# Masked attention with residual norms on one core: the softmax denominators' sums issued in each block's own step, y in two buffers, the norm's small product on GpSimd

## The chip, the core and the metric

The kernel runs on one core of a Trainium2 chip. A core has five engines that run side by side: TensorE (PE in the profile, its weight loads PEld), VectorE (DVE), ScalarE (ACT), GpSimd (POOL) and SyncE (SP, which only issues DMAs here). Each takes its instructions in the order of its queue, and an instruction that waits holds all behind it. DMA transfers are issued by SP or by GpSimd and run on 16 DMA engines. The metric is device time in microseconds, the median of three runs.

## The reference

For each of 8 frames of 2048 nodes with 256 channels the kernel computes eight-head attention (heads of 32) under an adjacency mask that all frames share, and then three layer norms with residuals and a two-layer network between them:

```python
qkv = jnp.einsum('fnc,ck->fnk', x, w_qkv)
scores = jnp.einsum('fnhd,fmhd->fhnm', q, k) / jnp.sqrt(D)
scores = jnp.where(adj > 0, scores, -1e9)
attn = jax.nn.softmax(scores, axis=-1)
t = jnp.einsum('fhnm,fmhd->fnhd', attn, v).reshape(F, N, C)
x1 = layernorm(x + t) * ln1_g + ln1_b
h = jax.nn.relu(x1 @ w1 + b1)
x2 = layernorm(x1 + h @ w2 + b2) * ln2_g + ln2_b
out = layernorm(x + x2)
```

All of it is float32.

## The kernel before

**Tiling.** A frame's queries are cut into four chunks `qc` of 512, the eight heads into two groups `g` of four, and the keys into 16 blocks `mb` of 128. One item `(f, qc, g, mb)` is one *block step*: there are 8 x 4 x 2 x 16 = 1024, unrolled in that order (L362). A *group* is the 16 steps of one `(f, qc, g)`. `tc.manual_schedule()` keeps every engine's instructions in the order in which the Python code makes them.

**A block step** `t` does four things, in this order. `advance(t)` puts one piece of waiting fill work in front (two where `mb` is odd, none where `mb` is 0). `scores(items[t + 2])` (L169) works two steps ahead: matmuls into PSUM, transposed, keys on the partitions; DVE adds the mask and writes the block's tile `p` (128 x 4 heads x 512 queries, 1 MB) to SBUF (L180); ACT takes exp in place (L182). `values(items[t])` (L186) adds this block's part of attention times V to a PSUM bank. Last, `denominators(t)` (L205) issues what the softmax denominators need. The pool `pp` has nine slots for `p`; a slot comes free when all that reads the tile has ended.

**Denominators before.** The sum over keys goes over partitions and over 16 blocks. Blocks 0 to 13 of a group make seven pairs: two steps after the even block, a DMA issued by GpSimd adds its tile onto the odd one's (L211); five steps after, GpSimd adds the pair to `acc` (the first two pairs make it, L218, the others L220: six additions). Blocks 14 and 15 stay as they are. `denominator` (L243), started five steps after block 15, contracts the three terms with a matrix of ones (L250), copies the result (L252), transposes it (L256), and takes the reciprocal (L260); L265 and L266 keep a running sum and minimum of the reciprocals, which at the end decide whether a slower, general path has to be run.

**The fill.** Work other than attention is written as generators that `yield` the number of steps to wait; `advance` runs the first that is due, and a generator that yields 0 lets the next one go. Denominators and tails are put at the head of the list (`urgent`), projections of the next frame and, in frame 0, the turning of the mask at its end. Where K and V of the next frame are not ready when its scores are due, the loop at L381 drives the fill until they are.

**The tail** of a query chunk (L268) runs from `state["y"]` being clear to its store: attention is transposed and divided into the tile `y` (L279, L280), x is added by a DMA that GpSimd issues (L284), three steps later comes a norm, then transposes (L294), the first layer (L303), the second (L312) with DVE's addition (L314), a norm, GpSimd's scaling (L317, L318), x again (L319), a norm, and the store (L322, on SP's queue). `state["y"]` is cleared once the store has been issued. `y` has one buffer.

**The norm** (L223): DVE takes mean and variance (L227, L228); GpSimd computes `rs`, one over the root of variance plus eps, in two small operations (L231, L232); two steps later DVE computes `nb = -mean * rs` (L235), and ACT normalizes in place with four activations (L237).

Of the kernel before, what the change touches and what calls it, by code (L numbers as in the profile page):

```python
# [10 lines left out]
F32 = mybir.dt.float32  # L11
# [4 lines left out]
ALU = mybir.AluOpType  # L16
AX = mybir.AxisListType

P = 128
H = 8  # L20
D = 32
CH = 512
# [1 line left out]

RS_MIN = 1e-19
RS_MAX = 1e25

MASKED = -57344.0  # L30

# [21 lines left out]
def fast_path(ctx, tc, cst, x, adj, out, RS):  # L53
    nc = tc.nc
    F, N, C = x.shape
    NCK, TPC, MB = N // CH, CH // P, N // P
# [7 lines left out]
    pp = ctx.enter_context(tc.tile_pool(name="pp", bufs=9))  # L64
    ap = ctx.enter_context(tc.tile_pool(name="ap", bufs=1))
    work = ctx.enter_context(tc.tile_pool(name="work", bufs=1))
    op = ctx.enter_context(tc.tile_pool(name="op", bufs=1))
    small = ctx.enter_context(tc.tile_pool(name="small", bufs=4))

# [97 lines left out]
    PT, O, OT, DT, ACC, RC = {}, {}, {}, {}, {}, {}  # L167
# [16 lines left out]
    LAST = MB - 1  # L184
# [14 lines left out]

    NPAIR = MB // 2 - 1
    ISSUE, ADD, SUM = 2, 5, 20

    def denominators(t):  # L205
        def block(back):
            return items[t - back] if 0 <= t - back < len(items) else (0, 0, 0, LAST)
        item = block(ISSUE)
        f, qc, g, mb = item
        if mb % 2 == 0 and mb // 2 < NPAIR:  # L210
            nc.gpsimd.dma_start(PT[f, qc, g, mb + 1], PT.pop(item), accum_op=ALU.add)  # L211
        f, qc, g, mb = block(ADD)
        grp, k = (f, qc, g), mb // 2
        if mb % 2 == 0 and 0 < k < NPAIR:
            pair = PT.pop((f, qc, g, mb + 1))
            if k == 1:
                ACC[grp] = ap.tile([P, 4, CH], F32, name="acc")
                nc.gpsimd.tensor_tensor(ACC[grp], PT.pop((f, qc, g, 1)), pair, ALU.add)  # L218
            else:
                nc.gpsimd.tensor_tensor(ACC[grp], ACC[grp], pair, ALU.add)  # L220


    def norm(t):  # L223
        mv = small.tile([P, TPC, nc.vector.BN_AGGR_DIM], F32, name="mv")
        for j in range(TPC):
            st = small.tile([P, nc.vector.BN_STATS_DIM], F32, name="st")
            nc.vector.bn_stats(st, t[:, j, :])  # L227
            nc.vector.bn_aggr(mv[:, j, :], st)  # L228
        yield 1
        rs = small.tile([P, TPC], F32, name="rs")  # L230
        nc.gpsimd.tensor_scalar(rs, mv[:, :, 1], EPS, 1.0, op0=ALU.add, op1=ALU.mult)  # L231
        nc.gpsimd.tensor_tensor(rs, rs, cst["mhalf"], ALU.pow)  # L232
        yield 2
        nb = small.tile([P, TPC], F32, name="nb")
        nc.vector.scalar_tensor_tensor(nb, mv[:, :, 0], -1.0, rs, op0=ALU.mult, op1=ALU.mult)  # L235
        for j in range(TPC):
            nc.scalar.activation(t[:, j, :], t[:, j, :], AF.Identity, bias=nb[:, j:j + 1], scale=rs[:, j:j + 1])  # L237
        yield 1
# [3 lines left out]

    def denominator(f, qc, g):  # L243
        grp = (f, qc, g)
        terms = [PT.pop((f, qc, g, LAST - 1)), PT.pop((f, qc, g, LAST)), ACC.pop(grp)]
        ps = bank()
        for n, term in enumerate(terms):
            for h in range(4):
                r = D * h
                nc.tensor.matmul(ps[r:r + D, :], cst["ones"], term[:, h, :], start=(n == 0), stop=(n == 2))  # L250
        dT = op.tile([P, CH], F32, name="dT")
        nc.scalar.copy(dT, ps)  # L252
        yield 1
        ps = bank()
        for j in range(TPC):
            nc.tensor.transpose(ps[:, j * P:(j + 1) * P], dT[:, j * P:(j + 1) * P], ident)  # L256
        if g == 0:
            RC[f, qc] = op.tile([P, TPC, H], F32, name="rc")
        rc = RC[f, qc]
        nc.vector.reciprocal(rc[:, :, 4 * g:4 * g + 4], ps.rearrange("p (j c) -> p j c", c=P)[:, :, ::D])  # L260
        if g == 0:
            return
        start(items.index((f, qc, g, LAST)) + SUM - MB + 3, tail(f, qc), urgent=True)
        rcf = rc.rearrange("p j h -> p (j h)")
        nc.vector.tensor_tensor(RS[:, 0, :], RS[:, 0, :], rcf, ALU.add)  # L265
        nc.vector.tensor_tensor(RS[:, 1, :], RS[:, 1, :], rcf, ALU.min)  # L266

    def tail(f, qc):  # L268
        while state["y"]:
            yield 0  # L270
        state["y"] = True
        rc = RC.pop((f, qc))
        xin = x[f, qc * CH:(qc + 1) * CH, :].rearrange("(j p) c -> p j c", p=P)
        y = work.tile([P, TPC, C], F32, name="y")
        for gg in range(2):
            oT = OT.pop((f, qc, gg))
            ps = bank()
            for j in range(TPC):
                nc.tensor.transpose(ps[:, j * P:(j + 1) * P], oT[:, j * P:(j + 1) * P], ident)  # L279
            nc.vector.tensor_tensor(y[:, :, gg * P:(gg + 1) * P].rearrange("p j (h d) -> p j h d", d=D),  # L280
                                    ps.rearrange("p (j h d) -> p j h d", h=4, d=D),
                                    rc[:, :, 4 * gg:4 * gg + 4, None].to_broadcast([P, TPC, 4, D]), ALU.mult)
            yield 1
        nc.gpsimd.dma_start(y, xin, accum_op=ALU.add)  # L284
        yield 3
        yield from norm(y)
        while state["turned"]:
            yield 0
        state["turned"] = True
        yT = work.tile([P, 2, CH], F32, name="turned")  # L290
        for a in range(2):
            ps = bank()
            for j in range(TPC):
                nc.tensor.transpose(ps[:, j * P:(j + 1) * P], y[:, j, a * P:(a + 1) * P], ident)  # L294
            nc.scalar.activation(yT[:, a, :], ps, AF.Identity, bias=cst["be1c"][:, a:a + 1], scale=cst["g1c"][:, a:a + 1])  # L295
            yield 1
        nc.gpsimd.tensor_tensor(y, y, rows(cst["g1r"]), ALU.mult)
        nc.gpsimd.tensor_tensor(y, y, rows(cst["be1b2r"]), ALU.add)
        hT = work.tile([P, 2, CH], F32, name="hT")
        for d in range(2):  # L300
            ps = bank()
            for a in range(2):
                nc.tensor.matmul(ps, w1s[:, a, d * P:(d + 1) * P], yT[:, a, :], start=(a == 0), stop=(a == 1))  # L303
            nc.scalar.activation(hT[:, d, :], ps, AF.Relu, bias=cst["b1s"][:, d:d + 1], scale=1.0)  # L304
            yield 1
        state["turned"] = False
        z = y
        for jj in range(0, TPC, 2):
            ps = bank()
            for j in range(jj, jj + 2):  # L310
                for d in range(2):
                    nc.tensor.matmul(ps[:, (j - jj) * C:(j - jj + 1) * C], hT[:, d, j * P:(j + 1) * P], w2s[:, d, :],  # L312
                                     start=(d == 0), stop=(d == 1))
            nc.vector.tensor_tensor(z[:, jj:jj + 2, :], ps.rearrange("p (b c) -> p b c", c=C), z[:, jj:jj + 2, :], ALU.add)  # L314
            yield 1
        yield from norm(z)
        nc.gpsimd.tensor_tensor(z, z, rows(cst["g2r"]), ALU.mult)  # L317
        nc.gpsimd.tensor_tensor(z, z, rows(cst["be2r"]), ALU.add)  # L318
        nc.gpsimd.dma_start(z, xin, accum_op=ALU.add)  # L319
        yield 5  # L320
        yield from norm(z)
        nc.sync.dma_start(out[f, qc * CH:(qc + 1) * CH, :].rearrange("(j p) c -> p j c", p=P), z)  # L322
        state["y"] = False
# [4 lines left out]
    def start(t, gen, urgent=False):  # L328
        fill.insert(0 if urgent else len(fill), [t, gen])
# [32 lines left out]
    for t, (f, qc, g, mb) in enumerate(items):  # L362
# [20 lines left out]
                t0 += 1  # L383
            scores(items[t + LEAD])
        values(items[t])
        denominators(t)
        if mb == LAST:
            start(t + SUM - MB + 1, denominator(f, qc, g), urgent=True)
    t = len(items)
    for i in range(ADD):  # L390
        denominators(t + i)
    while fill:
        t += 1
        advance(t)
# [125 lines left out]
def kernel(  # L520
# [15 lines left out]
    nc = tc.nc  # L536
    F, N, C = x.shape
    assert C == H * D == 2 * P and N % CH == 0
    NCK, TPC = N // CH, CH // P
# [32 lines left out]
    nc.gpsimd.memset(cst["ones"], 1.0)  # L572
    cst["mhalf"] = const.tile([P, TPC], F32, name="mhalf")
    nc.gpsimd.memset(cst["mhalf"], -0.5)
    RS = const.tile([P, 2, TPC * H], F32, name="RS")
    nc.gpsimd.memset(RS[:, 0, :], 0.0)
    nc.gpsimd.memset(RS[:, 1, :], 1.0)

    fast_path(tc, cst, x, adj, out, RS)

# [1 line left out]
    with tc.tile_pool(name="gd", bufs=1) as gd, \  # L582
            tc.tile_pool(name="gdp", bufs=1, space=bass.MemoryType.PSUM) as gdp:
        ok = gd.tile([P, 2], F32, name="ok")
        nc.vector.tensor_reduce(ok[:, 0:1], RS[:, 0, :], AX.X, ALU.add)
        nc.vector.tensor_reduce(ok[:, 1:2], RS[:, 1, :], AX.X, ALU.min)
        nc.vector.tensor_scalar(ok[:, 0:1], ok[:, 0:1], RS_MAX, None, op0=ALU.is_le)
        nc.vector.tensor_scalar(ok[:, 1:2], ok[:, 1:2], RS_MIN, None, op0=ALU.is_ge)
        ps = gdp.tile([2, 1], F32, name="okp")
        nc.tensor.matmul(ps, ok, cst["ones"][:, 0:1], start=True, stop=True)  # L590
        n_ok = gd.tile([2, 1], F32, name="nok")
# [39 lines left out]
```

## Time and profile before

| | |
|---|---|
| three runs | 4570.1, 4572.4, 4586.9 us; median 4572.44 |
| the profiled execution | 4558.5 us, its span 4556.7 us |
| granted TensorE clock in it, mean | 0.898 |
| first exp starts | 73.8 us |
| last exp starts | 4464.8 us |
| DMA queue that GpSimd issues to | 503.35 MB, 56.0% of 16 engines' span |

In the page's busy rows an engine's time is given as a share of the span. Rows of slices cut the span into 40 equal parts, a digit for each, in tenths; PEclk is the granted TensorE clock. In the answers on waits a row reads: engine, tile and line that waited, what ended the wait, total us, times, longest. In the groups of instructions: line, engine, operation, tiles, shapes, count, then busy us and mean ns, then the idle time before them and what ended most of it. A timeline row has the start in us, the duration, engine, line, tiles, count of merged instructions, and in brackets the idle time of the engine just before and what ended it. The answer on a single line has min/median/max of its durations in ns.

### The profile page before, as it was taken

Reading aid. Unit: us, or ns where it says so; the run is one execution under the profiler, and the core shown is the slowest. Engines: PE = TensorE matmul, PEld = TensorE weight load, DVE = VectorE, ACT = ScalarE, POOL = GpSimd, SP = SyncE. Lnnn points to the kernel's source line nnn. Section 1 sums busy time; section 2 is a strip of 40 time slices with the busy share of each in tenths; the row PEclk is TensorE's granted clock in tenths of the full one; section 3 lists DMA queues with packets and bytes.
Section 4 is the critical chain, followed back from the end, with each engine's and each line's share of the span. In section 5 each row is a group of like instructions: output and inputs, shape, how many; then the busy total and the mean of one; then the engine's idle time right before and its main releaser. Section 6 shows DMA issues by size and latency. Waiting matters only on the chain. (4 is left out here: it accounts for less than half of the span.)

```text
span 4556.7 us, 51690 instructions
## 1 busy us (share of the span) xinstructions
PE 3456.5 (76%) x20996; PEld 1038.2 (23%) x20996; DVE 2881.5 (63%) x3207; ACT 2458.0 (54%) x1953; POOL 2640.3 (58%) x1227
## 2 busy tenths in 40 slices
PE   7777778777777777777877777877778777787773
PEld 3122222212222222222221122221222222222221
DVE  3867547776476764766647765477655776567672
ACT  4665546555465554555545555455554555455552
POOL 1565546665466664765646755466645666456664
PEclk9998999889998899888998889898898988998886
DMA  5875756666476664776646765467754676556663
GB/s 145 177 156 131 155 105 123 135 140 143 101 144 140 123 139 99 145 149 135 122 104 137 147 148 112 97 137 146 148 107 96 140 145 142 116 105 140 139 130 61
DMA packets 148006, 592.59 MB, mean 130 GB/s; under 512 B 11184, under 2 KB 77872, under 8 KB 86320
## 3 DMA queue, kind: packets, MB, share of 16 engines
q0 software_dynamic: 98304, 503.35, 56.0%
q1 hardware_dynamic: 49456, 85.86, 5.9%
q8 instruction: 166, 2.72, 0.2%
q14 instruction: 80, 0.66, 0.0%
HBM read 98.44 MB, written 20.97 MB: 26 GB/s over the span
## 5 line engine op out<-in xcount | busy, mean ns | idle before, releaser
L180 DVE TENSOR_TENSOR p<-s,mask 128x1024 f32<-128x1024 f32 x2048 | 2409.2, 1218 | 1217.2 <-PE s L177 814.6
L182 ACT ACTIVATE p<-p 128x2048 f32<-128x2048 f32 x1024 | 1954.6, 1910 | 1580.4 <-DVE p L180 1391.9
L177 PE MATMUL s<-qT,kT 32*128 32x512 f32 x8192 | 1301.0, 708 | 511.8 <-DVE p L180 511.4
L220 POOL TENSOR_TENSOR acc<-acc,p 128x2048 f32<-128x2048 f32 x320 | 1523.0, 4759 | 238.2 <-DMA p<-p 231.9
L194 PE MATMUL x<-p,v 128*32 128x512 f32 x8192 | 1203.6, 663 | 14.8 <-ACT p L182 11.5
L211 POOL DMA_DIRECT2D p<-p x448 | 445.8, 1005 | 1020.7 <-PE x L194 866.4
L177 PEld LDWEIGHTS s<-qT,kT 32*128 32x128 f32 x8192 | 347.8, 199 | 1282.4 <-DVE p L180 1150.8
L194 PEld LDWEIGHTS x<-p,v 128*32 128x32 f32 x8192 | 167.2, 112 | 898.7 <-issue 649.4
L218 POOL TENSOR_TENSOR acc<-p 128x2048 f32<-128x2048 f32 x64 | 302.7, 4730 | 111.8 <-DMA p<-p 111.8
L145 PE MATMUL x<-turned,wqkv 128*128 128x512 f32 x480 | 267.2, 685 | 92.1 <-ACT kT L147 50.1
L237 ACT ACTIVATE y<-y,nb,rs 128x256 f32<-128x256 f32 x384 | 198.4, 587 | 118.1 <-DVE nb L235 118.1
L227 DVE BATCH_NORM_STATS2 st<-y 128x6 f32<-128x256 f32 x384 | 153.8, 401 | 88.1 <-DMA y<-in_x_dram 88.1
L303 PE MATMUL x<-turned,w1s 128*128 128x512 f32 x256 | 130.6, 633 | 47.8 <-DVE rc L260 24.8
L280 DVE TENSOR_TENSOR y<-x,rc 128x512 f32<-128x512 f32 x64 | 44.0, 688 | 189.9 <-DMA out_dram<-y 176.7
L284 POOL DMA_DIRECT2D y<-in_x_dram x32 | 42.5, 1328 | 188.2 <-DVE y L280 152.5
L145 PEld LDWEIGHTS x<-turned,wqkv 128*128 128x128 f32 x480 | 90.7, 209 | 266.3 <-ACT kT L147 90.2
L235 DVE SCALAR_TENSOR_TENSOR nb<-mv,rs 128x4 f32<-128x4 f32 x96 | 141.5, 1474 | 14.3 <-POOL rs L232 14.3
L157 PE MATMUL x<-wqkv,turned 128*128 128x256 f32 x448 | 119.7, 413 | 39.8 <-ACT v L159 22.3
L250 PE MATMUL x<-p,ones 128*32 128x512 f32 x1024 | 129.3, 625 | 25.9 <-ACT turned L295 13.5
L279 PE MATMUL x<-ident,oT 128*128 128x128 f32 x256 | 55.1, 352 | 121.7 <-DVE y L280 120.6
L312 PE MATMUL x<-w2s,hT 128*128 128x256 f32 x512 | 127.6, 392 | 3.6 <-DVE rc L260 1.1
L317 POOL TENSOR_TENSOR y<-y,g2r 128x1024 f32<-128x1024 f32 x32 | 75.8, 2368 | 87.4 <-ACT y L237 87.4
(69 smaller groups left out, 1638.3 us busy)
## 6 DMA issues: line engine op xcount, KB each, us to landing
p<-p POOLq DMA_DIRECT2D x448, 1024.0 KB, 7.6
y<-in_x_dram POOLq DMA_DIRECT2D x64, 512.0 KB, 5.9
mask<-md SPq DMA_DIRECT2D x28, 1024.0 KB, 11.0
in<-in_x_dram SPq DMA_DIRECT2D x32, 512.0 KB, 13.8
in<-in_adj_dram SPq DMA_DIRECT2D x32, 512.0 KB, 4.9
out_dram<-y SPq DMA_DIRECT2D x32, 512.0 KB, 6.9
md<-mask SPq DMA_DIRECT2D x4, 1024.0 KB, 5.1
wqkv<-in_L_gnn_w_qkv_dram SPq DMA_DIRECT2D x1, 768.0 KB, 4.2
```

The lines of the kernel that those rows point to most:

```text
L145: nc.tensor.matmul(ps, wqkv[:, a, k0 + g * P:k0 + (g + 1) * P], xT[:, a, :], start=(a == 0), stop=(a == 1))
L177: nc.tensor.matmul(ps2[half][:, j, :], KT[f, mb // TPC][r:r + D, g, (mb % TPC) * P:(mb % TPC + 1) * P], QT[f, qc][r:r + D, g, :], start=Tr ...
L180: nc.vector.tensor_tensor(pt[:, 2 * half:2 * half + 2, :], ps, MK[f, qc][:, mb, None, :].to_broadcast([P, 2, CH]), ALU.add)
L182: nc.scalar.activation(pt, pt, AF.Exp, scale=1.0 / math.sqrt(D))
L194: nc.tensor.matmul(O[grp][r:r + D, :], V[f, mb // TPC][:, mb % TPC, g * P + r:g * P + r + D], PT[item][:, h, :], start=(mb == 0), stop=(mb ...
L211: nc.gpsimd.dma_start(PT[f, qc, g, mb + 1], PT.pop(item), accum_op=ALU.add)
L218: nc.gpsimd.tensor_tensor(ACC[grp], PT.pop((f, qc, g, 1)), pair, ALU.add)
L220: nc.gpsimd.tensor_tensor(ACC[grp], ACC[grp], pair, ALU.add)
L227: nc.vector.bn_stats(st, t[:, j, :])
L235: nc.vector.scalar_tensor_tensor(nb, mv[:, :, 0], -1.0, rs, op0=ALU.mult, op1=ALU.mult)
L237: nc.scalar.activation(t[:, j, :], t[:, j, :], AF.Identity, bias=nb[:, j:j + 1], scale=rs[:, j:j + 1])
L303: nc.tensor.matmul(ps, w1s[:, a, d * P:(d + 1) * P], yT[:, a, :], start=(a == 0), stop=(a == 1))
```

## The change

**Denominators.** `denominators(t)` with its delays gives way to `add_up(item)`, called in the block's own step. Blocks 0, 1, 4, 7, 9, 12 and 14 are added up by GpSimd in `acc`, six additions, each issued in the step of its block. Blocks 2, 5, 8, 11 and blocks 3, 6, 10, 13 make two chains: the DMA of a later block of a chain adds its tile onto the chain's first, so the tiles of blocks 2 and 3 hold their slots until the denominator. Block 15 stays alone. `denominator` now starts four steps after block 15 and contracts four terms. The tail starts one step earlier than before.

**Running bounds.** They are taken of the denominators themselves, in PSUM, in each head group, not of the reciprocals once for both; the limits are turned over to match.

**y.** It comes from a pool of two buffers of its own. `state["y"]` stays: one tail at a time. Four steps instead of three lie between the first addition of x and its norm.

**Norm.** `nb` is made by GpSimd, a product and a scaling by -1, right after `rs`.

```diff
+    yp = ctx.enter_context(tc.tile_pool(name="yp", bufs=2))
...
-    NPAIR = MB // 2 - 1
-    ISSUE, ADD, SUM = 2, 5, 20
...
+    POOLED = (0, 1, 4, 7, 9, 12, 14)
+    CHAINS = ((2, 5, 8, 11), (3, 6, 10, 13))
+    SUM = 4
+
+    def add_up(item):
         f, qc, g, mb = item
+        grp = (f, qc, g)
+        for chain in CHAINS:
+            if mb in chain[1:]:
+                nc.gpsimd.dma_start(PT[f, qc, g, chain[0]], PT.pop(item), accum_op=ALU.add)
+        if mb == POOLED[1]:
+            ACC[grp] = ap.tile([P, 4, CH], F32, name="acc")
+            nc.gpsimd.tensor_tensor(ACC[grp], PT.pop((f, qc, g, POOLED[0])), PT.pop(item), ALU.add)
+        elif mb in POOLED[2:]:
+            nc.gpsimd.tensor_tensor(ACC[grp], ACC[grp], PT.pop(item), ALU.add)
...
         nc.gpsimd.tensor_tensor(rs, rs, cst["mhalf"], ALU.pow)
+        nb = small.tile([P, TPC], F32, name="nb")
+        nc.gpsimd.tensor_tensor(nb, mv[:, :, 0], rs, ALU.mult)
+        nc.gpsimd.tensor_scalar(nb, nb, -1.0, 1.0, op0=ALU.mult, op1=ALU.mult)
         yield 2
-        nb = small.tile([P, TPC], F32, name="nb")
-        nc.vector.scalar_tensor_tensor(nb, mv[:, :, 0], -1.0, rs, op0=ALU.mult, op1=ALU.mult)
...
-        terms = [PT.pop((f, qc, g, LAST - 1)), PT.pop((f, qc, g, LAST)), ACC.pop(grp)]
+        terms = [PT.pop((f, qc, g, LAST))] + [PT.pop((f, qc, g, chain[0])) for chain in CHAINS] + [ACC.pop(grp)]
...
-        nc.vector.reciprocal(rc[:, :, 4 * g:4 * g + 4], ps.rearrange("p (j c) -> p j c", c=P)[:, :, ::D])
-        if g == 0:
-            return
-        start(items.index((f, qc, g, LAST)) + SUM - MB + 3, tail(f, qc), urgent=True)
-        rcf = rc.rearrange("p j h -> p (j h)")
-        nc.vector.tensor_tensor(RS[:, 0, :], RS[:, 0, :], rcf, ALU.add)
-        nc.vector.tensor_tensor(RS[:, 1, :], RS[:, 1, :], rcf, ALU.min)
+        den = ps.rearrange("p (j c) -> p j c", c=P)[:, :, ::D]
+        nc.vector.reciprocal(rc[:, :, 4 * g:4 * g + 4], den)
+        nc.vector.tensor_tensor(RS[:, 0], RS[:, 0], den, ALU.add)
+        nc.vector.tensor_tensor(RS[:, 1], RS[:, 1], den, ALU.min)
+        if g == 1:
+            start(items.index((f, qc, g, LAST)) + SUM + 2, tail(f, qc), urgent=True)
...
-        y = work.tile([P, TPC, C], F32, name="y")
+        y = yp.tile([P, TPC, C], F32, name="y")
...
         nc.gpsimd.dma_start(y, xin, accum_op=ALU.add)
-        yield 3
+        yield 4
...
-        denominators(t)
+        add_up(items[t])
         if mb == LAST:
-            start(t + SUM - MB + 1, denominator(f, qc, g), urgent=True)
+            start(t + SUM, denominator(f, qc, g), urgent=True)
```

More of the change, by code (lines that the diff above doesn't have):

```diff
@@ L23 @@
 EPS = 1e-5
-RS_MIN = 1e-19
-RS_MAX = 1e25
+SUM_MIN = 1e-25
+SUM_MAX = 1e19
 MASKED = -57344.0
@@ L198, in values @@
             nc.scalar.copy(OT[grp], O.pop(grp))
-    NPAIR = MB // 2 - 1
-    ISSUE, ADD, SUM = 2, 5, 20
[L205 to L208, printed above, removed]
-        f, qc, g, mb = item
[L210 to L220, printed above, removed]
+    POOLED = (0, 1, 4, 7, 9, 12, 14)
+    CHAINS = ((2, 5, 8, 11), (3, 6, 10, 13))
+    SUM = 4
+    def add_up(item):
+        f, qc, g, mb = item
+        grp = (f, qc, g)
[7 more added lines that the diff above has]
+            nc.gpsimd.tensor_tensor(ACC[grp], ACC[grp], PT.pop(item), ALU.add)
     def norm(t):
@@ L249, in denominator @@
                 r = D * h
-                nc.tensor.matmul(ps[r:r + D, :], cst["ones"], term[:, h, :], start=(n == 0), stop=(n == 2))
+                nc.tensor.matmul(ps[r:r + D, :], cst["ones"], term[:, h, :], start=(n == 0), stop=(n == 3))
         dT = op.tile([P, CH], F32, name="dT")
@@ L385, in fast_path @@
         values(items[t])
-        denominators(t)
+        add_up(items[t])
         if mb == LAST:
-            start(t + SUM - MB + 1, denominator(f, qc, g), urgent=True)
+            start(t + SUM, denominator(f, qc, g), urgent=True)
     t = len(items)
-    for i in range(ADD):
-        denominators(t + i)
     while fill:
@@ L574 @@
     nc.gpsimd.memset(cst["mhalf"], -0.5)
-    RS = const.tile([P, 2, TPC * H], F32, name="RS")
-    nc.gpsimd.memset(RS[:, 0, :], 0.0)
-    nc.gpsimd.memset(RS[:, 1, :], 1.0)
+    RS = const.tile([P, 2, TPC, H // 2], F32, name="RS")
+    nc.gpsimd.memset(RS[:, 0], 0.0)
+    nc.gpsimd.memset(RS[:, 1], 1.0)
     fast_path(tc, cst, x, adj, out, RS)
@@ L584 @@
         ok = gd.tile([P, 2], F32, name="ok")
[L585 to L588, printed above, removed]
+        nc.vector.tensor_reduce(ok[:, 0:1], RS[:, 0].rearrange("p a b -> p (a b)"), AX.X, ALU.add)
+        nc.vector.tensor_reduce(ok[:, 1:2], RS[:, 1].rearrange("p a b -> p (a b)"), AX.X, ALU.min)
+        nc.vector.tensor_scalar(ok[:, 0:1], ok[:, 0:1], SUM_MAX, None, op0=ALU.is_le)
+        nc.vector.tensor_scalar(ok[:, 1:2], ok[:, 1:2], SUM_MIN, None, op0=ALU.is_ge)
         ps = gdp.tile([2, 1], F32, name="okp")
```

## The prediction

> **What bounds the kernel now.** I read the page's busy rows and slices first, then the waits of each engine, then the timeline where the longest of them stand.
>
> ```profile
> PE 3456.5 (76%) x20996; PEld 1038.2 (23%) x20996; DVE 2881.5 (63%) x3207; ACT 2458.0 (54%) x1953; POOL 2640.3 (58%) x1227
> PEclk9998999889998899888998889898898988998886
> ```
>
> No engine is full: the five hand work around in a ring, and what ends late in the ring sets the time. A block step needs two mask additions of DVE (L180), one exp of ACT (L182), and on PE scores and values.
>
> ```profile
> 1509.07 2.36 DVE L180 TENSOR_TENSOR p<-s,mask 128x1024 f32<-128x1024 f32 x2 [2.04 <-PE s L177]
> 1510.44 1.14 PE L177 MATMUL s<-qT,kT 32*128 32x512 f32 x8
> 1511.51 1.06 PE L194 MATMUL x<-p,v 128*32 128x512 f32 x8
> 1511.52 1.91 ACT L182 ACTIVATE p<-p 128x2048 f32<-128x2048 f32 x1 [1.83 <-DVE p L180]
> ```
>
> DVE's 2.36 us stand against 2.20 on PE, so a bare step takes about 2.5 us: 1024 of them make 2560 of the 4556.7 us. The rest, some 2000 us, is work of the fill (denominators, tails, projections) put in front of the scores on PE, or waits at the head of an engine's queue. A wait at the head of DVE's queue holds every mask addition behind it.
>
> ```profile
> DVE p L180 <- PE s L177: 814.6, 486, 19.2
> DVE y L280 <- DMA out_dram<-y: 176.7, 30, 8.7
> DVE st L227 <- DMA y<-in_x_dram: 88.1, 17, 13.3
> DVE p L180 <- POOL acc L220: 50.1, 33, 3.1
> DVE p L180 <- DMA p<-p: 31.1, 21, 3.3
> ...
> PEld x L250 <- POOL acc L220: 53.9, 16, 16.1
> ```
>
> The first row is PE's fill. The others are waits for a buffer or a sum, and those the change touches.
>
> **Part by part.** Terms are made against the profiled execution (4558.5 us, its span 4556.7); the median of the three runs, 4572.4, is 14 us higher, and the forecast is the median less the sum.
>
> *y in two buffers.* A tail clears its flag when its store is issued, and the next one starts a step later, so its first write meets the store on its way.
>
> ```profile
> 1465.41 1.12 PE L279 MATMUL x<-ident,oT 128*128 128x128 f32 x4
> 1472.54 0.69 DVE L280 TENSOR_TENSOR y<-x,rc 128x512 f32<-128x512 f32 x1 [6.37 <-DMA out_dram<-y]
> 1473.28 0.66 PE L279 MATMUL x<-ident,oT 128*128 128x128 f32 x4 [4.31 <-DVE y L280]
> 1474.41 2.09 PE L177 MATMUL s<-qT,kT 32*128 32x512 f32 x8 [0.47 <-DVE p L180]
> ```
>
> DVE was free at 1466.17 and the transposes ended at 1466.53: of 6.37 us only 0.36 stay, PE being next. Over 30 waits: 176.7 - 30 x 0.36 = 166, nearly all on the path, since PE stood still for 4.31 us too. I take **-165** (0 if the new tile got the old slot, -177 at most).
>
> *Small norm product.* It leaves DVE for GpSimd.
>
> ```profile
> L235 DVE SCALAR_TENSOR_TENSOR nb<-mv,rs x96: 145/164/4484, 238.5 to 4548.8; 128x4 f32<-128x4 f32 x96
> ...
> L235 DVE SCALAR_TENSOR_TENSOR nb<-mv,rs 128x4 f32<-128x4 f32 x96 | 141.5, 1474 | 14.3 <-POOL rs L232 14.3
> L232 POOL TENSOR_TENSOR rs<-rs,mhalf 128x4 f32<-128x4 f32 x96 | 99.7, 1039 | 8.0
> L231 POOL TENSOR_SCALAR rs<-mv 128x4 f32<-128x4 f32 x96 | 18.2, 190 | 159.5 <-DVE mv L228 156.2
> ...
> 1496.42 4.83 POOL L220 TENSOR_TENSOR acc<-acc,p 128x2048 f32<-128x2048 f32 x1
> 1497.11 4.16 DVE L235 SCALAR_TENSOR_TENSOR nb<-mv,rs 128x4 f32<-128x4 f32 x1
> 1501.36 2.08 ACT L237 ACTIVATE y<-y,nb,rs 128x256 f32<-128x256 f32 x4 [2.13 <-DVE nb L235]
> 1502.46 2.09 PE L177 MATMUL s<-qT,kT 32*128 32x512 f32 x8 [4.21 <-DVE p L180]
> ```
>
> A product of 128x4 lasts 164 ns at the median and 1474 at the mean: begun during a GpSimd add it ends when the add does (1501.27 against 1501.25). The stall is 96 x (1.474 - 0.164) = 126 us, and mask additions queue behind it. But such a step also holds 2.08 + 1.91 us on ACT, longer than DVE's 2.36, which remain. I take two thirds, **-80** (0 to -126). GpSimd takes two more small operations: each between 0.19 (L231) and 1.04 (L232, a power); nearest to a product and a scaling is 0.19, so 96 x 0.38 = 36 us, at most 200. They stand in front of the next block's add; the activations that need them come two steps on, over 5 us, which hides them, and GpSimd idles for 1916 us. Uncovered, each would hold ACT, so exp, by that much.
>
> *Sums.* Seven pair transfers per group become six links of two chains; the six adds stay. GpSimd issues 64 fewer DMAs.
>
> ```profile
> L211 POOL DMA_DIRECT2D p<-p x448 | 445.8, 1005 | 1020.7 <-PE x L194 866.4 <-ACT turned L295 54.8 <-ACT p L182 33.8
> L220 POOL TENSOR_TENSOR acc<-acc,p 128x2048 f32<-128x2048 f32 x320 | 1523.0, 4759 | 238.2 <-DMA p<-p 231.9 <-PE x L194 6.1
> DMA to landing us min/median/max: 6.9/7.6/15.5
> ...
> 1478.00:1490.00 12.00, 8.63 (x71) 1.96 (x72) 11.31 (x17) 7.64 (x4) 11.84 (x7) 1.00 0.98 190
> ```
>
> (The last row is a stretch of bare steps: PE, PEld, DVE, ACT, POOL busy, clock, DMA share.) GpSimd at 11.84 of 12 us and the DMA engines at 0.98 say that bare steps run at the limit of both. Now a pair is added only after its landing; afterwards an add needs exp alone, and a link writes a chain head whose values are long read, so the waits for PE (866.4) and for landings before an add (231.9) go off GpSimd. Against this: heads 2 and 3 and block 15 hold three of nine p slots into the next group, and each link waits at the head of GpSimd's queue for the link before. Links are three or four steps apart, 7.5 us or more in bare steps, 13 at the mean step of 4.45 (4556.7 / 1024), against 7.6 to land. Of 50.1 + 31.1 + 53.9 = 135 us of waits for slots and sums I take half off, less what the end holds: **-60** (-135 to +345, the slower rival).
>
> A rule speaks against this. The Trainium skill, "DMA: Bandwidth & Descriptors", section "Rules for kernel authors": an accumulating DMA reads its destination and writes it later, so one touching the same bytes must wait for the earlier one's semaphore. Now each transfer has its own destination and hardly waits for another (no run here shows a chain); by the rule alone every link is serial, and the sum would lose the -60 and more.
>
> *Fourth denominator term.* Eight more matmul records per group.
>
> ```profile
> 1518.45 0.13 PEld L250 LDWEIGHTS x<-p,ones 128*32 128x32 f32 x4 [0.30 <-issue]
> 1518.88 0.13 PEld L250 LDWEIGHTS x<-p,ones 128*32 128x32 f32 x4 [0.30 <-issue]
> ```
>
> Four records take 0.43 us, a term 0.86, 64 groups 55 us, in front of scores on a PE that DVE then waits for: **+55** (up to 110 at half clock).
>
> *Running bounds.* L265 and L266 run for each half: 64 more of
>
> ```profile
> L265 DVE TENSOR_TENSOR RS<-RS,rc 128x32 f32<-128x32 f32 x32 | 6.1, 192 | 1.1
> ```
>
> or **+12**; they now read PSUM and a half as long row (0 to +24).
>
> *Order.* Following the yields: a tail is still one period of 32 steps; the store and the next tail's first transposes now share step 9; the first accumulating load has four steps, not three, to land. Of 88.1 us in 17 waits, 17 x 2.5 = 43 could go; some belong to the second load: **-35** (0 to -88). The g = 0 denominator now runs in step 3 together with the first norm's activations. Alone, these made a step of 2.08 + 1.91 against DVE's 2.36, 1.6 us over; beside 3.4 us of denominator matmuls they are hidden: up to 32 x 1.6 = 51, taken **-40** (0 to -51). On SP's queue the store moves a few steps later, past no load that is due sooner; mask and x loads stay at their steps. Projections still forced out at a frame's end are the same pieces in another mix: nothing.
>
> *End.*
>
> ```profile
> 4484.82 1.94 PE L250 MATMUL x<-acc,ones 128*32 128x512 f32 x8 [15.24 <-POOL acc L220]
> 4494.83 0.69 DVE L280 TENSOR_TENSOR y<-x,rc 128x512 f32<-128x512 f32 x1 [4.05 <-DMA out_dram<-y]
> ```
>
> The last sum is ready earlier, but the tail before it still has to finish: **-12** (0 to -19).
>
> *Clock.* After 4.21 us of idle the eight score records took 2.09 us, a few steps on 1.14: 0.95 each. At most 78 such stalls go (30, and 48 waits of ACT for L235): 0 to -74; many lie under DVE, so **-20**.
>
> The Trainium skill, "TensorE: Matmul & The Clock Gate", "What's actually happening", says that an idle window of about 3.4 us halves the clock until about as long a busy one has passed. The 2.09 against 1.14 agrees; by it each stall slows some 3.4 us of work, 1.7 us lost, an estimate of 133 us, and the sum would be some 110 us larger.
>
> Sum: -165 - 80 - 60 + 55 + 12 - 35 - 40 - 12 - 20 = **-345**, and 4572.4 - 345 is about 4227: I forecast **4225**.
>
> **Rivals.** *(1) The clock comes back in full.* After that stall the values were slow too:
>
> ```profile
> 1504.48 1.94 PE L194 MATMUL x<-p,v 128*32 128x512 f32 x8
> ```
>
> 0.88 us over their 1.06, so 1.83 per stall and 143 for 78. Were most of it on the path, some 85 would come on top of my 20: **4140**. For it: the clock row at 8 in nearly half the slices. Against: DVE is the longer in bare steps.
>
> *(2) y still waits* (the edit doesn't do what it says), its tile being handed the slot just stored from: the 165 stay, **4390**. Against: with nine p slots, 448 transfers made DVE wait only 21 times, so slots long free are taken first.
>
> *(3) Chain waits back up GpSimd.* Four links per group wait for their forerunner, rs and the products sit behind, ACT waits for them in front of exp. It gives back the 60 and the 35, and a third of the 80: about 120, **4345**. For it: landings up to 15.5 us. Against: the mean step.
>
> *(4) Slower: slots starve.* At a group's start seven of nine p slots are held, and two links' slots must land before DVE may write. Free of cost up to about 4.5 steps, 11.3 us in bare steps. If landings there were all at the 15.5 us seen at most, two links cost 2 x 4.2 us x 64 = 538, **4765**; it decides from 345 / 128 = 2.7 us per link. Against: 64 fewer transfers on the engines, and the median of 7.6.
>
> **How the numbers follow.** Forecast 0.57 (own range 4150 to 4300), (1) 0.14, (2) 0.10, (3) 0.13, (4) 0.06. The range 4110 to 4390 leaves out (4), some of (2) and the far end of (1), under 2 in 10. Half a per cent is about what a measurement of this kernel can tell from no change: faster 0.91, same 0.03, slower 0.06.
>
> **What would show it.** L280 no longer waits for the store; no DVE instruction lasts microseconds for 128x4; ACT's wait for it is gone and none for GpSimd's product takes its place; GpSimd's waits for PE x L194 go, waits for DMA p<-p at the links stay below 3 us each; L250 at 2048 plus 512 records; clock above 0.9. I am wrong if DVE p waits for DMA p<-p or POOL by hundreds of us, or if PE's fill takes up what the waits gave.

## The result, and the profile after

The changed kernel takes 4097.1 us at the median of four runs (4093.1 to 4098.0) against 4579.7 before: 0.894 of the time, 95% interval 0.892 to 0.897. It is faster, as forecast, but by 10.5% and not by 7.6%, and 13 us below the low end of the range.

The page of the changed kernel gives its span, the busy times with their shares of it, and the granted clock in 40 slices. Lines are numbered anew: L181 is the mask addition, L183 exp, L212 a chain's link, L215 and L217 GpSimd's sum, L248 the denominator, L277 the first write of y, L281 the first load of x, L224 the norm's statistics, L235 its activations.

```profile
span 4091.3 us, 52692 instructions
PE 3308.0 (81%) x21508; PEld 1011.5 (25%) x21508; DVE 2745.5 (67%) x3175; ACT 2443.2 (60%) x1953; POOL 2624.4 (64%) x1355
PEclk9899899999999999999999999999999999999996
```

DVE lost 136 us of busy time, the stretched products; the other 330 us of the shorter span are idle time that it no longer has. The waits of its queue (what waited, for what, total us, times, longest):

```profile
DVE p L181 <- PE s L178: 827.2, 536, 16.6
DVE st L224 <- DMA y<-in_x_dram: 144.3, 25, 15.4
...
DVE p L181 <- DMA p<-p: 19.2, 9, 4.4
DVE y L277 <- PE x L276: 16.5, 16, 1.3
```

No row waits for the store any more, and GpSimd's sums do not hold up DVE. One wait has grown: the norm's statistics wait 144.3 us for x, 88.1 before. GpSimd's queue has a new row:

```profile
POOL p L212 <- DMA p<-p: 153.8, 52, 8.7
POOL acc L215 <- PE x L248: 147.0, 12, 16.7
```

The first is links waiting for their forerunners, 52 of 384, 3.0 us each. The second, GpSimd waiting to overwrite `acc` until the last denominator has read it, I had not seen coming, and it turned out to matter. One sign of the prediction is not met: it said that no wait of ACT for GpSimd's product would take the old one's place, and one of 62.1 us does, most of it (46.8 us in four waits) after the last exp:

```profile
ACT y L235 <- POOL nb L232: 62.1, 11, 15.6
```

The timeline of a step with the denominator and the first norm's activations shows what a good step looks like now:

```profile
1773.71 2.76 PE L248 MATMUL x<-p,ones 128*32 128x512 f32 x24
1776.28 1.04 PE L248 MATMUL x<-acc,ones 128*32 128x512 f32 x8
1777.25 1.14 PE L178 MATMUL s<-qT,kT 32*128 32x512 f32 x8
1777.39 0.58 ACT L250 COPY dT<-x 128x512 f32<-128x512 f32 x1
1777.87 2.07 ACT L235 ACTIVATE y<-y,nb,rs 128x256 f32<-128x256 f32 x4
1778.53 2.35 DVE L181 TENSOR_TENSOR p<-s,mask 128x1024 f32<-128x1024 f32 x2 [3.16 <-PE s L178]
1780.98 1.91 ACT L183 ACTIVATE p<-p 128x2048 f32<-128x2048 f32 x1 [1.03 <-DVE p L181]
```

ACT's copy and four activations end at 1779.94, while DVE is still at the mask additions that exp waits for: here they cost nothing.

### The profile page after: what moved, and what is told of

Its sections match the earlier page's. It is cut to its first block, busy times and chain, and to the rows that moved or that the text cites. A ratio compares the mean times of both kernels' runs of the same rounds, so it can differ in the third digit from the quotient of the medians.

```text
span 4091.3 us, 52692 instructions
## 1 busy us (share of the span) xinstructions
PE 3308.0 (81%) x21508; PEld 1011.5 (25%) x21508; DVE 2745.5 (67%) x3175; ACT 2443.2 (60%) x1953; POOL 2624.4 (64%) x1355
## 5 line engine op out<-in xcount | busy, mean ns | idle before, releaser
L181 DVE TENSOR_TENSOR p<-s,mask 128x1024 f32<-128x1024 f32 x2048 | 2410.5, 1219 | 968.3 <-PE s L178 827.2
L183 ACT ACTIVATE p<-p 128x2048 f32<-128x2048 f32 x1024 | 1951.4, 1910 | 1326.1 <-DVE p L181 1135.6
L217 POOL TENSOR_TENSOR acc<-acc,p 128x2048 f32<-128x2048 f32 x320 | 1505.2, 4704 | 201.5 <-ACT p L183 196.8
L178 PE MATMUL s<-qT,kT 32*128 32x512 f32 x8192 | 1230.3, 671 | 472.9 <-DVE p L181 472.9
L195 PE MATMUL x<-p,v 128*32 128x512 f32 x8192 | 1140.1, 630 | 28.7 <-ACT p L183 28.4
L215 POOL TENSOR_TENSOR acc<-p 128x2048 f32<-128x2048 f32 x64 | 290.9, 4546 | 655.0 <-ACT p L183 508.0
L212 POOL DMA_DIRECT2D p<-p x384 | 362.9, 977 | 362.9 <-ACT p L183 166.3
L146 PE MATMUL x<-turned,wqkv 128*128 128x512 f32 x480 | 249.2, 645 | 50.9 <-ACT kT L148 29.0
L224 DVE BATCH_NORM_STATS2 st<-y 128x6 f32<-128x256 f32 x384 | 153.9, 401 | 144.3 <-DMA y<-in_x_dram 144.3
L235 ACT ACTIVATE y<-y,nb,rs 128x256 f32<-128x256 f32 x384 | 198.3, 588 | 62.1 <-POOL nb L232 62.1
L248 PE MATMUL x<-p,ones 128*32 128x512 f32 x1536 | 183.1, 610 | 15.8 <-ACT qT L148 14.8
L158 PE MATMUL x<-wqkv,turned 128*128 128x256 f32 x448 | 112.9, 395 | 31.1 <-ACT v L160 10.1
L228 POOL TENSOR_SCALAR rs<-mv 128x4 f32<-128x4 f32 x96 | 18.4, 191 | 147.9 <-DVE mv L225 144.2
L309 PEld LDWEIGHTS x<-w2s,hT 128*128 128x128 f32 x512 | 92.0, 189 | 69.1 <-ACT hT L301 31.1
L229 POOL TENSOR_TENSOR rs<-rs,mhalf 128x4 f32<-128x4 f32 x96 | 99.5, 1036 | 8.0
L158 PEld LDWEIGHTS x<-wqkv,turned 128*128 128x128 f32 x448 | 81.6, 192 | 77.3 <-ACT qT L148 28.5
L291 PE MATMUL x<-ident,y 128*128 128x128 f32 x256 | 44.6, 294 | 66.9 <-ACT turned L292 46.4
```

The lines of the kernel that those rows point to most:

```text
L146: nc.tensor.matmul(ps, wqkv[:, a, k0 + g * P:k0 + (g + 1) * P], xT[:, a, :], start=(a == 0), stop=(a == 1))
L158: nc.tensor.matmul(ps[:, (j - jj) * C:(j - jj + 1) * C], xT[:, a, j * P:(j + 1) * P], wqkv[:, a, 2 * C:], start=(a == 0), stop=(a == 1))
L178: nc.tensor.matmul(ps2[half][:, j, :], KT[f, mb // TPC][r:r + D, g, (mb % TPC) * P:(mb % TPC + 1) * P], QT[f, qc][r:r + D, g, :], start=Tr ...
L181: nc.vector.tensor_tensor(pt[:, 2 * half:2 * half + 2, :], ps, MK[f, qc][:, mb, None, :].to_broadcast([P, 2, CH]), ALU.add)
L183: nc.scalar.activation(pt, pt, AF.Exp, scale=1.0 / math.sqrt(D))
L195: nc.tensor.matmul(O[grp][r:r + D, :], V[f, mb // TPC][:, mb % TPC, g * P + r:g * P + r + D], PT[item][:, h, :], start=(mb == 0), stop=(mb ...
```

## The experiments

The question was why the terms, taken one by one, came out 130 us short. Theory A: they were right, and the clock that comes back with fewer stalls (rival 1) is the rest. Theory B: the order of the pieces in the steps, a small term of mine, is the rest. Every time below is a median of four runs (a_order: ten), with before measured beside it on the same chip at 4575 to 4581 us; ratios are to that, with their 95% intervals. A run's name stands in front of its time (b_ is built on the kernel before, a_ on the changed one, but for b_sums, whose diff is against the changed one); line numbers differ by a few from run to run.

### Each part alone, added to before

*Two buffers for y.*

```diff
-        y = work.tile([P, TPC, C], F32, name="y")
+        y = yp.tile([P, TPC, C], F32, name="y")
```

> Before with y in two buffers, nothing else. Theory A (the terms of the prediction were right, the clock gives the rest): 165 us from the wait plus up to 85 us of clock, 4330 to 4410, granted clock up by 0.01 or more. Theory B (the order of the fill's pieces gives the rest): the 165 us alone, about 4410. Both: L280 no longer waits for the store.

b_y2: 4504.7 us, ratio 0.984 (0.980 to 0.987): 73 us, not 165, and the clock did not move (0.898). Neither theory's number. DVE's waits in this run say where the rest went:

```profile
DVE st L228 <- DMA y<-in_x_dram: 175.9, 31, 13.2
```

The wait for the store is gone, 176.7 us, and the wait for x, one piece on in the same queue, has doubled from 88.1. The load itself got slower. These are GpSimd's wait for y in front of that load, and the load's time to land, before and then in this run:

```profile
POOL y L284 <- DVE y L280: 152.5, 25, 17.0
DMA to landing us min/median/max: 5.6/9.2/15.5
...
POOL y L285 <- DVE y L281: 80.4, 13, 11.9
DMA to landing us min/median/max: 6.0/13.8/18.0
```

With one y the load went out 5.1 us at the median after GpSimd had issued the pair transfer ahead of it, with two 0.1 us. That the closeness of the two is what slows the load is argued here; a_load, further down, moves the transfer ahead.

*The product on GpSimd.*

```diff
-        yield 2
         nb = small.tile([P, TPC], F32, name="nb")
-        nc.vector.scalar_tensor_tensor(nb, mv[:, :, 0], -1.0, rs, op0=ALU.mult, op1=ALU.mult)
+        nc.gpsimd.tensor_tensor(nb, mv[:, :, 0], rs, ALU.mult)
+        nc.gpsimd.tensor_scalar(nb, nb, -1.0, 1.0, op0=ALU.mult, op1=ALU.mult)
+        yield 2
```

> Before with the norm's small product on GpSimd, nothing else. Theory A: 80 to 126 us plus some clock, 4410 to 4490. Theory B: 80 us or less, 4490 to 4530, since ACT's own activations hold those steps.

b_nb: 4534.1 us, ratio 0.990 (0.985 to 0.994): 44 us: less than theory B's 80, though 4 us above the range that it gave. ACT's activations are not the whole reason. DVE's waits for slots of `p` grow from 81.2 us (50.1 for GpSimd's additions and 31.1 for pair transfers) to 143.8 (92.3 and 51.5), half of the 126 us that the stall was worth:

```profile
DVE p L180 <- POOL acc L220: 92.3, 41, 4.1
```

*The sums, at before's steps.* This is the changed kernel without the two edits above and with the steps put back:

```diff
-            start(t + SUM, denominator(f, qc, g), urgent=True)
+            start(t + SUM + 1, denominator(f, qc, g), urgent=True)
...
-            start(items.index((f, qc, g, LAST)) + SUM + 2, tail(f, qc), urgent=True)
+            start(items.index((f, qc, g, LAST)) + SUM + 3, tail(f, qc), urgent=True)
...
-        yield 4
+        yield 3
```

> Before with the three running sums, the four terms and the running bounds of the denominators, but denominator, tail and first norm at before's steps. By the prediction's terms -60 + 55 + 12 = about 0 us: 4550 to 4590 under both theories; over 4650 if chains starve the slots, under 4500 if waits for slots were worth more than I took.

b_sums: 4711.6 us, ratio 1.029 (1.025 to 1.033): slower, by 134 us, and not for want of slots, for which DVE waits 44.2 us. GpSimd's waits in this run:

```profile
POOL acc L214 <- PE x L246: 582.9, 38, 28.2
...
POOL p L211 <- DMA p<-p: 109.5, 56, 8.6
```

`acc` is one tile. Issued in its own step, the first addition of a group stands at the head of GpSimd's queue in step 1, while the group before still needs `acc` until its denominator in step 4 or later. All that GpSimd issues waits behind it: links, additions, the load of x, the norm's small operations.

*The steps alone.*

```diff
-            start(t + SUM - MB + 1, denominator(f, qc, g), urgent=True)
+            start(t + SUM - MB, denominator(f, qc, g), urgent=True)
...
-        start(items.index((f, qc, g, LAST)) + SUM - MB + 3, tail(f, qc), urgent=True)
+        start(items.index((f, qc, g, LAST)) + SUM - MB + 2, tail(f, qc), urgent=True)
...
-        yield 3
+        yield 4
```

> Before with only the steps shifted: denominator one step earlier, tail with it, four steps for the first load of x. Theory A: 75 us or less, 4500 or more. Theory B: 130 to 170 us from the pieces that no longer share a step, 4410 to 4450, though the store now stands in the same step as the next tail's first write, which can take back up to 60 us of waiting for it.

b_order: 4349.8 us, ratio 0.950 (0.947 to 0.954): 228 us, three times theory A's bound and more than B's. And that with two waits that this order makes worse: the store's is 188.7 us, 176.7 before, and the denominator now often comes before GpSimd's sum is ready (201.8 us of PE's weight loads, 53.9 before). The timeline, at such a place:

```profile
1931.10 1.93 PE L250 MATMUL x<-acc,ones 128*32 128x512 f32 x8 [6.50 <-POOL acc L220]
1932.96 2.09 PE L177 MATMUL s<-qT,kT 32*128 32x512 f32 x8
...
1935.19 2.36 DVE L180 TENSOR_TENSOR p<-s,mask 128x1024 f32<-128x1024 f32 x2 [10.82 <-PE s L177]
```

PE waits 6.5 us for the sum at the head of its queue, the scores behind it, and DVE 10.8 us for them. The product, in turn, hardly suffers here:

```profile
L235 DVE SCALAR_TENSOR_TENSOR nb<-mv,rs 128x4 f32<-128x4 f32 x96 | 24.1, 251 | 15.8 <-POOL rs L232 15.8
```

251 ns at the mean, 1474 before: in this order 4 of the 96 products last longer than 0.4 us, 45 before.

### Each part taken out of the changed kernel

One y (the first diff reversed):

> The changed kernel with y in one buffer again. Theory A: 165 to 250 us slower than changed, 4262 to 4350. Theory B: about 165 us, and since the store and the next tail's first write share a step here, up to 60 more: 4262 to 4325.

a_y1: 4299.4 us, ratio 0.939 (0.936 to 0.942): 202 us slower than changed, within both. The store's wait is larger here than in the kernel before, and without the second buffer the load lands in 7.7 us at the median, against 16.9 in the changed kernel:

```profile
DVE y L276 <- DMA out_dram<-y: 298.2, 31, 14.6
DMA to landing us min/median/max: 5.9/7.7/19.1
```

The statistics wait 29.8 us for x in this run and 144.3 in the changed kernel: again a good part of the store's wait comes back at the load.

The product on DVE (the second reversed):

> The changed kernel with the small product back on DVE two steps after rs. Theory A: 80 to 150 us slower, 4177 to 4247. Theory B: less than 80, since the first norm's activations lie under the denominator's matmuls.

a_nb: 4226.2 us, ratio 0.922 (0.919 to 0.925): 129 us slower. Theory B had less than 80 and falls in this point: the product is slow again, 1342 ns at the mean.

```profile
L232 DVE SCALAR_TENSOR_TENSOR nb<-mv,rs 128x4 f32<-128x4 f32 x96 | 128.9, 1342 | 21.3 <-POOL rs L229 21.3
```

The steps as before (the third diff, with y and the product left changed):

> The changed kernel with denominator, tail and first load at before's steps. Theory A: 75 us slower at most, 4172 or less. Theory B: 130 to 170 us slower, 4227 to 4267, less what the wait for the first load of x (124 us in the changed kernel) changes.

a_order: 4584.3 us, ratio 1.001 (0.999 to 1.003): the whole gain is gone, 487 us, far beyond both theories. GpSimd waits 571.2 us for the denominator, DVE 204.4 us for slots and 283.8 for x:

```profile
2039.09 4.55 POOL L215 TENSOR_TENSOR acc<-p 128x2048 f32<-128x2048 f32 x1 [14.03 <-PE x L248]
```

The sums, leaving the other three parts (before with the steps, two y and the product on GpSimd); first without the product:

> Before with the steps shifted (b_order, 4350 us) and y in two buffers. If the second buffer is worth what the wait at L280 shows once the first load of x has its four steps: 188 us of waiting go, 4160 to 4200. If it is worth no more than alone on before (73 us): about 4275.

b_order_y2: 4228.5 us, ratio 0.925 (0.922 to 0.929): 121 us below b_order, between the two guesses. With it:

> The changed kernel but for the sums: before with shifted steps, y in two buffers and the product on GpSimd. In b_order_y2 (4228 us) the product took 555 ns at the mean on DVE, so 96 x 0.39 = 38 us at most can come from it: 4190 to 4228. The sums' own part in the changed kernel is then 90 to 130 us, the denominator's wait for GpSimd (241 us of PE's weight loads in b_order_y2) less their fourth term.

b_order_y2_nb: 4223.6 us, ratio 0.922 (0.918 to 0.925): with the old sums and the new steps the product brings nothing measurable (the denominator's wait for GpSimd's sum goes from 241.2 to 257.6 us), and the sums are worth 126 us once all else stands. The steps and the sums alone:

> The changed kernel with one y and the product on DVE: shifted steps and new sums alone. If the parts add up from here: 4097 + 202 + 129 = 4428, slower than b_order's 4350. If the sums are worth the denominator's wait that b_order shows (ACT dT waits 202.9 us for PE, which waits for the sum): 4150 to 4250.

a_y1_nb: 4401.8 us, ratio 0.962 (0.960 to 0.965): 52 us slower than b_order and 26 us below the first guess. The sums spare PE its wait for them, but the product's stalls are back (1455 ns at the mean), the store's wait grows to 256.5 us, and GpSimd waits 181.1 us for `acc`.

### What in the steps it is, and the one tile

Theory C: with before's steps the new sums lose by the wait for the one `acc`. The sum is made in block 1's own tile, and acc's memory is a tenth slot for p; the sum is the same:

```diff
-    pp = ctx.enter_context(tc.tile_pool(name="pp", bufs=9))
-    ap = ctx.enter_context(tc.tile_pool(name="ap", bufs=1))
+    pp = ctx.enter_context(tc.tile_pool(name="pp", bufs=10))
...
-            ACC[grp] = ap.tile([P, 4, CH], F32, name="acc")
-            nc.gpsimd.tensor_tensor(ACC[grp], PT.pop((f, qc, g, POOLED[0])), PT.pop(item), ALU.add)
+            ACC[grp] = PT.pop(item)
+            nc.gpsimd.tensor_tensor(ACC[grp], PT.pop((f, qc, g, POOLED[0])), ACC[grp], ALU.add)
```

> The kernel with before's steps (a_order, 4584 us) whose GpSimd sum is made in block 1's own tile instead of the one tile acc, with that tile's memory as a tenth slot for p. Theory C (with before's steps the first addition of a group waits at the head of GpSimd's queue, 571 us in all, for the denominator that still reads the only acc, and links, slots and the load of x queue behind it): that wait goes, and a good part of the loss with it, 4350 to 4480. Theory B (sharing a step is the loss, whatever GpSimd does): 4540 or more.

a_order_inpl: 4376.8 us, ratio 0.956 (0.955 to 0.958): 208 of the 487 us come back, as C has it. The edit does two things, though: DVE's waits for slots fall from 204.4 to 67.2 us too, and no run tells the one tile's share from the tenth slot's.

> The changed kernel with the sum in block 1's tile and ten slots. Theory C: GpSimd waits for the denominator only 147 us here, off the path mostly: 4060 to 4100. Theory B: no change, 4090 to 4105.

a_inpl: 4043.7 us, ratio 0.883 (0.881 to 0.884): 53 us faster than changed, more than I gave it: the wait of 147 us was in part on the path, or the tenth slot was worth it.

The load's four steps alone, on before:

> Before with four steps instead of three between the first load of x and its norm, which moves the whole tail against the denominator by some steps too. If the load's time is what counts: near b_order, 4350 to 4400. If the denominator's own step counts: less than half of the 228 us, 4470 to 4580.

b_y4: 4442.9 us, ratio 0.972 (0.970 to 0.973): 132 us, the larger part of b_order's 228; the earlier step of denominator and tail adds 93. That step alone, put back on the ten-slot kernel (a_order_inpl has both put back):

> a_inpl (4044 us) with denominator and tail a step later, the load's four steps kept; a_order_inpl, which has three steps for the load as well, took 4377. If the denominator's step is what counts: 4250 to 4380. If the load's steps count: 4040 to 4120.

a_sum5_inpl: 4194.8 us, ratio 0.917 (0.915 to 0.918): 151 us slower than a_inpl for the step, and 182 more in a_order_inpl for the load. So both count, in either kernel, and neither half of the guess is right alone.

The order's price can be read off before's timeline, at a step in which a denominator's transposes (L256) and a first layer (L303) follow each other:

```profile
1524.26 0.25 DVE L260 RECIPROCAL rc<-x 128x16 f32<-128x16 f32 x1
1524.56 1.98 PE L303 MATMUL x<-turned,w1s 128*128 128x512 f32 x4 [1.13 <-DVE rc L260]
1526.47 1.14 PE L177 MATMUL s<-qT,kT 32*128 32x512 f32 x8
1526.58 0.69 ACT L304 ACTIVATE hT<-x,b1s 128x512 f32<-128x512 f32 x1 [0.24 <-PE x L303]
1527.74 2.35 DVE L180 TENSOR_TENSOR p<-s,mask 128x1024 f32<-128x1024 f32 x2 [3.23 <-ACT hT L304]
```

Two pieces in one step share the one PSUM bank that is free for the fill. The second can't start before DVE has taken the reciprocal out of the first, which stands behind mask additions; the scores stand behind the second, and DVE then idles 3.23 us (its row names the end of `hT` at 1527.27; the scores that it adds the mask to end at 1527.61). In the changed kernel the transposes and the two halves of the first layer have steps of their own. The row for such waits in the kernel before, and then in b_order:

```profile
DVE p L180 <- ACT hT L304: 112.2, 35, 3.3
...
DVE p L180 <- ACT hT L304: 5.7, 1, 5.7
```

With the load's four steps alone (b_y4) it is 64.0 us. The statistics' wait for x goes from 88.1 us to 25.3 in that run and 20.0 in b_order, and DVE's wait for slots that GpSimd's additions hold from 50.1 to 19.0 and 7.0. The three together lose 218 us in b_order, against 228 of the time.

### The load of x, and a faster version

The remaining wait in the changed kernel, at the first norm:

```profile
1743.98 2.28 POOL L281 DMA_DIRECT2D y<-in_x_dram  x1
...
1761.11 0.43 DVE L224 BATCH_NORM_STATS2 st<-y 128x6 f32<-128x256 f32 x1 [6.37 <-DMA y<-in_x_dram]
```

It is issued between two links, here half a us after one, and takes 17 us to arrive. Two ways to have it sooner: a different block for the link ahead of it,

```diff
-    POOLED = (0, 1, 4, 7, 9, 12, 14)
-    CHAINS = ((2, 5, 8, 11), (3, 6, 10, 13))
+    POOLED = (0, 1, 4, 7, 10, 12, 14)
+    CHAINS = ((2, 5, 8, 11), (3, 6, 9, 13))
```

> The changed kernel with block 9 in the second chain and block 10 in GpSimd's sum, so that no chain transfer is issued in the step before the first load of x. If that load is late (landing 16.9 us at the median, 124 us of waiting) because it shares the engines with chain transfers around it: landing near 10 us, the wait under 60 us, 4000 to 4060. If it is late for another reason: 4090 to 4105.

a_load: 4086.5 us, ratio 0.892 (0.889 to 0.895). The load lands in 13.5 us, not near 10, and the first norm waits 47.1 us for it instead of 124.0 (all norms 66.5 instead of 144.3), so the link ahead was a part of its delay. But the time falls by 11 us only, near the second case: DVE's wait for slots rises from 19.2 to 100.9 us. A wait went where another was next. Or the load issued a step earlier:

```diff
-            yield 1
+            if gg == 0:
+                yield 1
         nc.gpsimd.dma_start(y, xin, accum_op=ALU.add)
-        yield 4
+        yield 5
```

> The changed kernel with the first load of x issued in the step of y's second half, one step earlier, norm where it was. If the load's wait (124 us at the first norm) is the one late thing left there: 4000 to 4050. If GpSimd then waits for y in front of an addition and slots come late in turn: 4080 to 4110.

a_now: 4047.5 us, ratio 0.884 (0.883 to 0.886): 50 us. With the ten slots:

> The changed kernel with both fixes: the sum in block 1's tile with ten slots (alone -53 us) and the first load of x a step earlier (alone -50 us). If they remove different waits: 3990 to 4010. If both only relieve GpSimd's queue ahead of that load: 4030 to 4045.

a_now_inpl: 4007.8 us, ratio 0.876 (0.874 to 0.877), 89 us faster than the changed kernel, of 103 for the two apart: they add up nearly in full. The statistics now wait 29.2 us, and the mean granted clock is 0.959.

## Why the prediction was wrong

**The step that failed** is the sum itself, with the paragraph on *order* as its worst term. I priced each edit against before's timeline, as if the others were not there, and gave the order 35 + 40 = 75 us. Alone on before it is worth 228, and without it the rest of the change is worth nothing (4584). The second is the term for y, "nearly all on the path": 165 forecast, 73 alone.

| part | forecast | alone, on before | last, on the other three |
|---|---|---|---|
| two y | -165 | -73 | -202 |
| product on GpSimd | -80 | -44 | -129 |
| sums, terms, bounds | -60 + 55 + 12 | +134 | -126 |
| steps | -35 - 40 | -228 | -487 |
| all four | -345 with end and clock | | -483 |

The four alone make -211, the four taken out -944, and the change -483: neither column adds up. Each part is worth more once the others stand; the waits named below show in part why.

**y in two buffers.** That the wait would go whole was right, and PE's transposes are next (16.5 us at L277), as forecast. What I left out is that the same wait set the load of x apart from the transfers around it: with the second buffer it lands later, and the norm, a fixed number of steps behind, waits for it. I had that wait on the page, 88.1 us, and counted it down, not up. On before, 176.7 us of waiting go and 87.8 come back, 89 net for 73 measured. In the changed kernel 298.2 go (the store and the next tail's first write share a step there) and 114.5 come back, 184 net for 202 measured: the second buffer is worth more at the end because there is more to wait for.

**Product.** The stall was read rightly. Two thirds was a guess for how much of it counts, and what it is worth depends on the order: 44, nothing (4228.5 to 4223.6), or 129 us. On before DVE then waits 62.6 us longer for slots that GpSimd's additions and transfers hold, which I had put at nothing; in the changed kernel, where it waits 19.2 us for slots, all of the stall counts. On GpSimd the two operations cost 38 us, 36 forecast:

```profile
L231 POOL TENSOR_TENSOR nb<-mv,rs 128x4 f32<-128x4 f32 x96 | 19.5, 203 | 7.5
L232 POOL TENSOR_SCALAR nb<-nb 128x4 f32<-128x4 f32 x96 | 18.5, 193 | 8.4
```

**Sums.** I said that the waits for PE go off GpSimd. Those of the pair transfers did, 866.4 us; but an addition moved to its own step now came before the last reader of the one `acc`, and I had looked at the slots of p and not at that tile. With the new steps it cost 53 us at most, with before's steps up to 208, the tenth slot included. What the sums gain is where I took only half: the denominator's wait, which the earlier step would make 202 to 241 us (PE's weight loads waiting for the sum in b_order and b_order_y2) if the sum were not ready by then. Of the two priced additions, the fourth term measured 52 us of PE's busy time (55 forecast) and the bounds 5 us of DVE's (12). The count of its records is 1536 plus 512, not the "2048 plus 512" of the prediction.

**Order.** I counted yields right, and saw that the activations would lie beside the denominator; they do. I did not price pieces that stop sharing a step. The step of denominator and tail (93 us on before, 151 at the end) and the load's step (132, 182) were each worth more than the 75 together.

**End.** -12 forecast. From the last exp's start to the end of the span it was 4556.7 - 4464.8 = 91.9 us, and is now 4091.3 - 4012.1 = 79.2:

```profile
L183 ACT ACTIVATE p<-p x1024: 1892/1911/1924, 73.2 to 4012.1; 128x2048 f32<-128x2048 f32 x171
```

**Rivals.** The clock did rise, 0.898 to 0.947, as in (1), and PE's busy time fell by 148.5 us though it has 512 more records, about the 143 us that (1) counted. How much of that was on the path no run separates: no part alone shows a gain by the clock without a wait that went, and two y alone left it at 0.898. The Trainium skill's rule of the idle window ("TensorE: Matmul & The Clock Gate", "What's actually happening") would have brought the forecast nearer, to about 4115 by the prediction's estimate, but whether for the right reason stays open. (2) and (4) did not happen. (3), GpSimd backing up, didn't happen at the links, where waiting stayed at 3.0 us each; it is what the changed kernel does with before's steps, where GpSimd waits 571.2 us for the one tile. The Trainium skill's rule that an accumulating DMA has to wait for an earlier one on the same bytes ("DMA: Bandwidth & Descriptors", "Rules for kernel authors") shows as the links' 52 waits and 153.8 us, without deciding the time.

## What to carry to other kernels

In a pipeline with in-order queues and a hand-made order, price the *schedule* that results, not the edits: write down which pieces share a step before and after, and for each freed wait ask what is due next in the same queue. When an operation is moved to an earlier step, look at every tile that it writes, and at who reads its last content and when; a single buffer far from the change can hold the whole queue. A part added to the start and the same part taken out of the finished change can differ several times over, so measure both. And a wait that goes may have kept two transfers apart: look at what is issued closer together without it.

## What was unexpected of the hardware

The 512 KB load of x that adds onto y took 9.2 us to land at the median before, and 16.9 issued half a us behind a 1 MB link and ahead of the next; both are issued by GpSimd. With the link ahead moved to another step it took 13.5, and with one y, where GpSimd waits 232.2 us in front of it, 7.7. A link takes 9.3 us at the median, 7.6 before, though there are fewer.

```profile
DMA to landing us min/median/max: 7.0/16.9/20.4
```

And the product of 128x4 on DVE ran at 153 ns at the median and 4675 at most in b_order, where 4 of 96 lasted longer than 0.4 us, against 285 and 4959 in a_nb, where 48 did: the instruction is the same, and what stands beside it on GpSimd is not.

```profile
L235 DVE SCALAR_TENSOR_TENSOR nb<-mv,rs x96: 150/153/4675, 243.4 to 4342.3; 128x4 f32<-128x4 f32 x96
L232 DVE SCALAR_TENSOR_TENSOR nb<-mv,rs x96: 152/285/4959, 250.8 to 4218.7; 128x4 f32<-128x4 f32 x96
```
